# Order of the first loads, split of the strip loads and the number of copy buffers in a fused attention and spline-MLP block

## Chip, cores and metric

The kernel runs on 1 core of one Trainium2 chip. The metric is device time in microseconds (us) of one execution. Before the change three runs took 575.83, 576.78 and 578.7 us, the median is 576.78 us. All data are float32.

## The reference

The block normalizes x (4 batches of 512 tokens, 512 channels) and adds two branches to it. The first is causal attention with 16 heads and a linear position bias. The second is a gated MLP (512 to 2048 to 512) whose three weight matrices are not given densely: each is a cubic interpolation of about 8,000 control points.

```
xn = layernorm(x)
attention: q, k, v = xn @ W + b;  softmax(q k' / sqrt(32) + slope * distance, causal) @ v;  @ Wo + bo
mlp:       gate_w, up_w, down_w = spline(control points)
           inner = silu(xn @ gate_w') * (xn @ up_w')        # 512 -> 2048
           down  = inner @ down_w'                          # 2048 -> 512
out = x + attention + mlp
```

## The kernel before

**Queues.** Every transfer is issued by SyncE (SP), in program order, and `in_order` (L379) fixes the order of all instructions of each engine as written. The transfers take eight semaphores in turn, so transfer n carries a wait for transfer n-8: SP issues it only when that one has landed, and everything behind it on SP waits too.

**Start (L562 to L572, L974 to L997).** `load_x` (L555) loads the four 128-token tiles of the first batch into `xp`, 256 KB each; `load_w` (L452) loads a whole 512x512 weight, 1 MB. SP issues: x tiles 0 and 1, Wv, x tiles 2 and 3, Wq, the bias columns, Wk and more. The first work on the data is written out by hand in L977 to L994. `first_stats` (L714) gives per-token statistics of one tile or two: `moments_of` (two VectorE instructions, L721 and L722), `root` (a VectorE instruction and a ScalarE square root, L726 and L727), `better` (five small VectorE instructions, L731 to L736). `norm` (L740) gives `go` (normalize on VectorE, L745) and `turn_it` (four TensorE transposes, L760, and a ScalarE copy into `xnT`, L761). `value(0, 0)` (`v0`, L797) multiplies token tile 0 by Wv in four steps c over the input channels (L807), two of them before the second tile is turned and two after it. Then q and k of the first heads follow (`project`, L767, matmuls at L776).

**Middle.** Attention of all four batches follows (about 20 us to 408 us). It also builds the MLP weights from control points, and it writes what the MLP needs of the normalized x to DRAM: sampled rows (`samples`) and moments of the stretches between them (`moments`).

**MLP stage (from about 408 us).** The MLP works on 32-row strips of features. `feat[b]` holds them for batch b and is loaded back from DRAM by `load_feat` (L523): four windows w, each of four strip transfers (11 rows of 4x512 values, L530), and after windows 1 and 3 four moment transfers (10 rows of 4x512, L537), 24 transfers in all. The first half `feat[:, 0]` holds windows 0 and 1, the second windows 2 and 3. Two buffers of `feat` take turns.

The order of the stage is written out as strings, one per batch (`plans`, L1197). Capital letters name steps: F0 and F1 issue the two parts of the strip loads for the next batch; G and U (V is U on the other set of PSUM banks) make a quarter of `gate` and of `inner`; m, R and S finish the batch before (moments of inner, down projection, last sum); L loads `res`, the sum of x and attention, 1 MB (L1146).

```
"F0 G0 P0 U0 F1 P1 G1 P2 U1 P3 G2 V2 G3 V3",
"F0 G0 m0:8 U0 L F1 m8:16 G1 T R0:6 U1 T R6:12 G2 R12:16 U2 S G3 V3",
"F0 G0 m0:8 U0 L F1 m8:16 G1 T R0:6 U1 T R6:12 G2 R12:16 U2 S G3 V3",
"G0 m0:8 U0 L m8:16 G1 T R0:6 U1 T R6:12 G2 R12:16 U2 S G3 V3",
"L M0:12 R0:2 M12:16 T R2:16 S",
```

I call these rows phase 0, 1, 2, 3 and the tail. `gate` (L1071) runs 16 matmuls (L1059) into four banks "g" and four ScalarE activations (L1074). `up` (L1076) runs 16 matmuls, four VectorE products into a tile of pool `intp` (L1081, six buffers), and four GpSimd copies into a tile `made` (L1082, two buffers). From `made` SP then moves every other row back into the other strip's place of `inner` (two transfers of 256 KB, L1086) and a few single rows into `lone` (L1091, L1095). The moments of a batch (`m`, L1106) read `inner` after these transfers have landed. S (`down_moments`, L1168) ends in four VectorE sums with `res` (L1186), which free the four banks "o" that V3 writes next, and in four output transfers (L1187).

Of the kernel before, what the change touches and what calls it, by code (L numbers as in the profile page):

```python
# [12 lines left out]
F32 = mybir.dt.float32  # L13
# [5 lines left out]
P = 128  # L19
B, S, D, H = 4, 512, 512, 16  # L20
# [3 lines left out]
NB = D // P  # L24
# [24 lines left out]
NW, NW4 = 11, 4  # L49
# [155 lines left out]
def window(g, w):  # L205

    return 8 * g + 129 * w - 1
# [187 lines left out]
def block_kernel(  # L395
# [17 lines left out]
    nc = tc.nc  # L413
# [35 lines left out]
    xtp = ctx.enter_context(tc.tile_pool(name="xt", bufs=3))  # L449
    wsb = {}  # L450

    def load_w(name, w, pool):  # L452
        wsb[name] = pool.tile([P, NB, D], F32, name=f"w{name}")
        nc.sync.dma_start(out=wsb[name], in_=w.rearrange("(c p) d -> p c d", p=P))


    bcol = wp.tile([P, 5, NHG], F32, name="bcol")
# [62 lines left out]
                if at == k:  # L520
                    nc.sync.dma_start(out=rows[s], in_=o[half * 64 : (half + 1) * 64])

    def load_feat(b, halves=range(2)):  # L523

        strip = lambda j: feat[b][j * Q32 : (j + 1) * Q32]
        turns = [(0, 2, 1, 3), (1, 3, 0, 2)]
        for w in range(2 * halves[0], 2 * halves[-1] + 2):
            for j in turns[w % 2]:
                rows = samples[b][window(j, w) + 1 :][:P].rearrange("(q r) d -> r q d", q=NB)
                nc.sync.dma_start(  # L530
                    out=strip(j)[w % 2 * NW : (w % 2 + 1) * NW, w // 2], in_=rows[:NW]
                )
            if w % 2:
                rows = moments[b].rearrange("(q r) d -> r q d", q=NB)
                for j in turns[0]:
                    at = (2 * j + w // 2) * 2 * NST
                    nc.sync.dma_start(  # L537
                        out=strip(j)[2 * NW :, w // 2], in_=rows[at : at + 2 * NST]
                    )


    with ExitStack() as att:
        attw = att.enter_context(tc.tile_pool(name="attw", bufs=1))
# [11 lines left out]
        def load_x(b, tiles=range(NB)):  # L555
            if tiles[0] == 0:
                xpt[b] = xpp.tile([P, NB, D], F32, name="xp")
            for t in tiles:
                r = (b * NB + t) * P
                nc.sync.dma_start(out=xpt[b][:, t], in_=xpf[r : r + P, :])  # L560

        for k in range(2):  # L562
            nc.gpsimd.memset(lone[k], 0.0)
            nc.gpsimd.memset(edge[k], 0.0)
        load_x(0, range(2))
        load_w("v", Wvp, attw)
        load_x(0, range(2, NB))
        load_w("q", Wqp, attw)
        nc.sync.dma_start(out=bcol, in_=cols)
# [15 lines left out]
            out=dist[:, S - P :],  # L585
            in_=dist[:, S - P :],
# [127 lines left out]
        def first_stats(t0, n):  # L714


            r = rstd[:, t0 : t0 + n]

            def moments_of(t):
                st = stat.tile([P, 6], F32, name="st")  # L720
                nc.vector.bn_stats(st, xpt[0][:, t])  # L721
                nc.vector.bn_aggr(mean[:, t], st)  # L722

            def root():
                variance[t0] = var = stat.tile([P, NB], F32, name="var")[:, :n]
                nc.vector.tensor_scalar_add(var, mean[:, t0 : t0 + n, 1], EPS)  # L726
                nc.scalar.activation(r, var, AF.Sqrt)  # L727

            def better():
                inv = stat.tile([P, NB], F32, name="inv")[:, :n]  # L730
                nc.vector.reciprocal(inv, r)  # L731
                nw = stat.tile([P, NB], F32, name="nw")[:, :n]
                nc.vector.tensor_tensor(nw, inv, inv, ALU.mult)
                nc.vector.tensor_tensor(nw, nw, variance[t0], ALU.mult)
                nc.vector.tensor_scalar(nw, nw, -0.5, 1.5, ALU.mult, ALU.add)
                nc.vector.tensor_tensor(r, inv, nw, ALU.mult)  # L736

            return *(lambda t=t: moments_of(t) for t in range(t0, t0 + n)), root, better

        def norm(b, t):  # L740
            def go():
                j = b * NB + t
                xn = tp.tile([P, D], F32, name="xn", bufs=2)
                ready[b, t] = xn
                nc.vector.tensor_scalar(  # L745
                    xn,
                    xpt[b][:, t],
                    mean[:, j, 0:1],
                    rstd[:, j : j + 1],
                    ALU.subtract,  # L750
                    ALU.mult,
                )

            def turn_it():
                xn = ready.pop((b, t))
                if t == 0:
                    xnT[b] = xtp.tile([P, NB, S], F32, name="xnT", bufs=2)
                ps = ps_m.tile([P, NB, P], F32, name="mm")
                for cb in range(NB):
                    nc.tensor.transpose(ps[:, cb, :], xn[:, cb * P : (cb + 1) * P], ident)  # L760
                nc.scalar.copy(xnT[b][:, :, t * P : (t + 1) * P], ps)  # L761

            return go, turn_it
# [33 lines left out]
        def value(b, t):  # L797

            ps = []

            def go(chunks=range(NB)):
                if t == 0 and chunks[0] == 0:
                    vals[b] = vp.tile([P, NB, D], F32, name="v")
                if chunks[0] == 0:
                    ps.append(ps_m.tile([P, D], F32, name="mm"))
                for c in chunks:
                    nc.tensor.matmul(  # L807
                        ps[0],
                        lhsT=xnT[b][:, c, t * P : (t + 1) * P],
                        rhs=wsb["v"][:, c, :],  # L810
                        start=(c == 0),
                        stop=(c == NB - 1),
                    )
                if chunks[-1] == NB - 1:
                    nc.vector.tensor_copy(vals[b][:, t, :], ps[0])

            return go
# [159 lines left out]
        one, two, three = first_stats(0, 1), first_stats(1, 1), first_stats(2, 2)  # L977
        norms = [norm(0, t) for t in range(NB)]
        v0, q0, k0 = value(0, 0), project("q", 0, 0, 2), project("k", 0, 0, 2)
        for step in (one[0], one[1], two[0], one[2], norms[0][0], two[1], norms[0][1]):  # L980
            step()
        v0(range(2))
        for step in (two[2], norms[1][0], *three[:3], norms[1][1]):
# [61 lines left out]
    featp = ctx.enter_context(tc.tile_pool(name="feat", bufs=1))  # L1045
    midp = ctx.enter_context(tc.tile_pool(name="midp", bufs=1))
    actp = ctx.enter_context(tc.tile_pool(name="actp", bufs=NB + 1))
    madep = ctx.enter_context(tc.tile_pool(name="made", bufs=2))
    intp = ctx.enter_context(tc.tile_pool(name="intp", bufs=6))
    ps_g = ctx.enter_context(tc.tile_pool(name="ps_g", bufs=NB, space=PSUM))  # L1050
    ps_o = ctx.enter_context(tc.tile_pool(name="ps_o", bufs=NB, space=PSUM))

# [18 lines left out]
    def gate(b, q):  # L1071
        for k, ps in enumerate(product(b, q, 0, ps_g, "g")):
            acts[k] = actp.tile([P, S], F32, name="act")
            nc.scalar.activation(acts[k], ps, AF.Silu)  # L1074
# [56 lines left out]
    def add_moments(b, n):  # L1131

        u, t, turned, steps = around[b]
        if not turning[b]:
            turning[b] = True
            for k in range(NB - 1, 0, -1):
                nc.scalar.copy(turned[:ND, k], t[ND:, k])
                nc.scalar.copy(turned[ND:, k], t[:ND, k])
        for k, part in [steps.popleft() for _ in range(min(n, len(steps)))]:
            e = NE - 1 - k  # L1140
            nc.vector.tensor_tensor(u[e][:ND], u[e + 1][:ND], part[:ND], ALU.add)
            nc.vector.tensor_tensor(u[k][ND:], u[k - 1][ND:], part[ND:], ALU.add)
# [62 lines left out]
    def carry_out(b, steps):  # L1205
        for step in steps.split():
            kind, which = step[0], step[1:]
            tiles = range(*map(int, which.split(":"))) if ":" in which else None
            if kind == "G":
                gate(b, int(which))  # L1210
            elif kind == "U":
                up(b, int(which))
            elif kind == "V":
                up(b, int(which), ps_o, "o")
            elif kind == "P":
                last[int(which)][1]()
                if int(which) == 0:
                    last[3][0]()
            elif kind == "M":
                inner_moments(b - 1, tiles, ps_g, "g")  # L1220
            elif kind == "m":
                inner_moments(b - 1, tiles, ps_o, "o")
            elif kind == "F":
                if int(which) == 0:
                    feat[b + 1] = (keep if b % 2 else featp).tile([P, 2, NB, S], F32, name="feat")
                load_feat(b + 1, [int(which)])
            elif kind == "T":
                add_moments(b - 1, 3)
            elif kind == "R":
                down_values(b - 1, tiles, ps_o, "o")  # L1230
            elif kind == "L":
                load_res(b - 1)
            else:
                down_moments(b - 1)

    for b, steps in enumerate(plans):
        carry_out(b, steps)
# [47 lines left out]
```

## Time and profile before

| | |
|---|---|
| runs, median (lowest to highest) | 576.78 us (575.83 to 578.7) |
| profiled execution, its own time | 573.35 us |
| its span from first to last instruction | 571.6 us |
| VectorE busy | 355.3 us (62%) |
| ScalarE busy | 295.8 us (52%) |
| GpSimd busy | 184.8 us (32%) |
| granted TensorE clock | 1.0 |
| transfers | 67.73 MB, mean 118 GB/s |

The profile is one execution. Its time is 573.35 us, 3.4 us below the median of the runs; 1.75 us of it lie outside the span. Times in the views are us from the start of the span. In the timeline a row gives start, length, engine, line, operation, tiles and count; `[idle before <-releaser]` gives how long the engine had stood and what ended it. fp32 matmuls appear as two records each. The trace also holds the moment at which every part of a transfer raised its semaphore; where I say that a transfer landed, it is the last of these.

### The profile page before, as it was taken

How to read it: one execution, taken by the hardware profiler on the slowest of the kernel's cores; microseconds unless marked ns; L12 is line 12 of the kernel's file. 1: busy time of each engine (PE TensorE's matmuls, PEld its weight loads, DVE VectorE, ACT ScalarE, POOL GpSimd, SP SyncE). 2: the span in 40 equal slices, each digit the busy share in tenths (PEclk: the TensorE clock that was granted, in tenths of full speed). 3: DMA queues.
4: the chain of work that ended last, by engine and by line, in shares of the span. 5: the costliest groups of instructions: out<-in, count | busy, mean ns of one | idle time of the engine just before them, and what ended most of it. 6: DMA issues, size and time to landing. Idle time of an engine off the chain costs nothing.

```text
span 571.6 us, 11202 instructions
## 1 busy us (share of the span) xinstructions
PE 560.7 (98%) x4012; PEld 276.7 (48%) x4012; DVE 355.3 (62%) x990; ACT 295.8 (52%) x782; POOL 184.8 (32%) x332
## 2 busy tenths in 40 slices
PE   6999999999999999999999999999999999999997
PEld 4645554544455555444655555555535334333343
DVE  5169998897587785637554545556244573854746
ACT  2366766565357556554756576677514412623323
POOL 2034534253134343222422442443124133113220
PEclk9999999999999999999999999999999999999999
DMA  8942346316453640211020004703546575785344
GB/s 285 344 91 75 73 127 192 108 40 204 128 158 110 193 160 0 66 38 75 2 76 18 1 2 94 128 1 85 129 131 172 119 187 189 130 194 187 115 151 162
DMA packets 34344, 67.73 MB, mean 118 GB/s; under 512 B 5648, under 2 KB 5648, under 8 KB 33776
## 3 DMA queue, kind: packets, MB, share of 16 engines
q1 hardware_dynamic: 34288, 67.01, 41.7%
q8 instruction: 32, 0.52, 0.4%
q14 instruction: 24, 0.20, 0.1%
HBM read 42.35 MB, written 15.29 MB: 101 GB/s over the span
## 4 chain that ended last, share of the span: by engine, by line
PE 87%; DVE 5%; ACT 4%; DMA 3%; issue 1%; SPq 1%; DVEq 0%
PE mm L776 18%; PE mm L891 11%; PE mm L807 10%; PE g L1059 9%; PE mm L475 7%; PE s L834 7%; PE o L1160 6%; PE c L905 5%; PE o L1106 3%; PE o L1177 3%; PE o L475 3%; ACT p L863 2%; PE mm L503 2%; PE o L1059 2%; DMA wv<-in_Wvp_dram 1%; DVE p L847 1%
## 5 line engine op out<-in xcount | busy, mean ns | idle before, releaser
L878 POOL TENSOR_SCALAR p<-p,inv 128x128 f32<-128x128 f32 (+3 forms) x256 | 142.5, 576 | 257.0 <-DVE inv L876 246.8
L863 ACT ACTIVATE p<-p,low 128x128 f32<-128x128 f32 (+3 forms) x256 | 140.7, 552 | 45.9 <-DVE low L847 45.5
L847 DVE CUSTOM_DVE_ANT_0 p<-s,dist 128x128 f32<-128x128 f32 (+3 forms) x256 | 109.2, 482 | 36.2 <-PE s L834 35.3
L891 PEld LDWEIGHTS mm<-ident,p 128*128 128x128 f32 x640 | 71.0, 141 | 40.4 <-issue 25.5
L891 PE MATMUL mm<-ident,p 128*128 128x128 f32 x640 | 89.0, 278 | 1.2 <-ACT pT L896 0.7
L896 ACT COPY pT<-mm 128x512 f32<-128x512 f32 x96 | 55.3, 581 | 53.9 <-PE mm L891 53.6
L1082 POOL COPY made<-inner 128x512 f32<-128x512 f32 x64 | 38.9, 636 | 108.7 <-DVE inner L1081 65.1
L1074 ACT ACTIVATE act<-g 128x512 f32<-128x512 f32 x64 | 33.2, 602 | 61.5 <-PE g L1059 61.5
L807 PE MATMUL mm<-wv,xnT 128*128 128x512 f32 x128 | 58.1, 595 | 2.3 <-DMA wv<-in_Wvp_dram 2.3
L776 PE MATMUL mm<-xnT,wk 128*128 128x512 f32 (+1 forms) x136 | 59.3, 579 | 0.2 <-ACT xnT L761 0.2
L776 PE MATMUL mm<-xnT,wq 128*128 128x512 f32 (+1 forms) x136 | 58.0, 569 | 0.3 <-ACT pT L896 0.2
L1059 PE MATMUL g<-feat,wT 32*128 32x512 f32 x432 | 57.9, 611 | 0.0
L834 PE MATMUL s<-kT,qT 32*128 32x512 f32 (+3 forms) x512 | 51.1, 468 | 0.3
L894 DVE COPY pT<-mm 128x512 f32<-128x512 f32 x64 | 43.6, 687 | 9.1 <-PE mm L891 8.6
L863 ACT ACTIVATION_READ_ACCUMULATOR p<-p,low 128x1 f32 x256 | 48.4, 189 | 0.0
L1081 DVE TENSOR_TENSOR inner<-g,act 128x512 f32<-128x512 f32 x44 | 27.3, 683 | 31.3 <-issue 15.2
L475 PE MATMUL mm<-ctxT,wo 128*128 128x512 f32 x88 | 40.0, 597 | 0.0
L1059 PEld LDWEIGHTS g<-feat,wT 32*128 32x128 f32 x432 | 23.4, 184 | 32.0 <-issue 19.3
L905 PE MATMUL c<-pT,v 128*32 128x128 f32 (+3 forms) x512 | 37.8, 436 | 0.0
L776 PEld LDWEIGHTS mm<-xnT,wk 128*128 128x128 f32 x136 | 24.5, 189 | 25.3 <-issue 21.9
L776 PEld LDWEIGHTS mm<-xnT,wq 128*128 128x128 f32 x136 | 24.7, 190 | 23.5 <-issue 22.3
L807 PEld LDWEIGHTS mm<-wv,xnT 128*128 128x128 f32 x128 | 23.0, 190 | 26.1 <-issue 26.0
(100 smaller groups left out, 556.0 us busy)
## 6 DMA issues: line engine op xcount, KB each, us to landing
inner<-made SPq DMA_DIRECT2D x32, 256.0 KB
feat<-samples SPq DMA_DIRECT2D x64, 88.0 KB
xp<-in_xp_dram SPq DMA_DIRECT2D x16, 256.0 KB
samples<-xnT SPq DMA_DIRECT2D x4, 1024.0 KB
feat<-in_coef_dram SPq DMA_DIRECT2D x8, 512.0 KB
feat<-in_rowpts_dram SPq DMA_DIRECT2D x32, 128.0 KB
xt<-in_xT_dram SPq DMA_DIRECT2D x16, 256.0 KB
mid<-xt SPq DMA_DIRECT2D x16, 256.0 KB
```

The source lines that it names most:

```text
L475: nc.tensor.matmul(ps, lhsT=wsb["o"][:, c, r * P : (r + 1) * P], rhs=ctxT[b][:, c, :], start=(c == 0), stop=(c == NB - 1),)
L776: nc.tensor.matmul(ps[0][:, tokens], lhsT=wsb[name][:, c, hg * P : (hg + 1) * P], rhs=xnT[b][:, c, tokens], start=(c == 0), stop=(c == NB ...
L807: nc.tensor.matmul(ps[0], lhsT=xnT[b][:, c, t * P : (t + 1) * P], rhs=wsb["v"][:, c, :], start=(c == 0), stop=(c == NB - 1),)
L834: nc.tensor.matmul(banks[b, hg][j][:, at : at + (k + 1) * P], lhsT=qk[b, hg, "q"][rows, k * P : (k + 1) * P], rhs=qk[b, hg, "k"][rows, : ( ...
L847: nc.vector.tensor_tensor_reduce(out=p[:, j, :nk], in0=ps[j], in1=dist[:, S - nk :], scale=-SLOPES[hg * NG + j], scalar=BIG, op0=ALU.add, ...
L863: nc.scalar.activation(p[:, j, :nk], p[:, j, :nk], AF.Exp, bias=low[:, j : j + 1], scale=-1.0, accum_out=total[:, j : j + 1],)
L878: nc.gpsimd.tensor_scalar(p[:, j, :nk], p[:, j, :nk], inv[:, j : j + 1], 1.0, ALU.mult, ALU.mult)
L891: nc.tensor.transpose(ps[:, j, :], p[:, j, c * P : (c + 1) * P], ident)
L894: nc.vector.tensor_copy(out, ps)
L896: nc.scalar.copy(out, ps)
L905: nc.tensor.matmul(ps[j * HD : (j + 1) * HD, c * P :], lhsT=vals[b][:, c, hg * P + j * HD : hg * P + (j + 1) * HD], rhs=w[:, j, :], start= ...
L1059: nc.tensor.matmul(ps[k], lhsT=wT[rows, q, 2 * w + part, :], rhs=feat[b][rows, part, q, :], start=(part == 0), stop=(part == 1),)
```

## The change

Three things change. The first loads come in another order: x tile 0, the first half of Wv (input channels 0 to 255), x tile 1, the second half of Wv, x tiles 2 and 3, Wq and so on; the hand-written first VectorE work finishes tile 0 before it begins tile 1. The strip loads of a batch are split in windows 0, 1, 2 (F0: 16 transfers instead of 12) and window 3 (F1: 8 instead of 12). `made` gets a third buffer and `intp` five instead of six; both tiles are of one size.

```diff
-    def load_w(name, w, pool):
-        wsb[name] = pool.tile([P, NB, D], F32, name=f"w{name}")
-        nc.sync.dma_start(out=wsb[name], in_=w.rearrange("(c p) d -> p c d", p=P))
+    def load_w(name, w, pool, chunks=slice(0, NB)):
+        if chunks.start == 0:
+            wsb[name] = pool.tile([P, NB, D], F32, name=f"w{name}")
+        rows = w.rearrange("(c p) d -> p c d", p=P)
+        nc.sync.dma_start(out=wsb[name][:, chunks], in_=rows[:, chunks])
...
-    def load_feat(b, halves=range(2)):
+    def load_feat(b, windows=range(NW4)):
...
-        for w in range(2 * halves[0], 2 * halves[-1] + 2):
+        for w in windows:
...
-        load_x(0, range(2))
-        load_w("v", Wvp, attw)
+        load_x(0, range(1))
+        load_w("v", Wvp, attw, slice(0, 2))
+        load_x(0, range(1, 2))
+        load_w("v", Wvp, attw, slice(2, NB))
         load_x(0, range(2, NB))
...
-        for step in (one[0], one[1], two[0], one[2], norms[0][0], two[1], norms[0][1]):
+        for step in (*one, norms[0][0], *two[:2], norms[0][1]):
...
-    madep = ctx.enter_context(tc.tile_pool(name="made", bufs=2))
-    intp = ctx.enter_context(tc.tile_pool(name="intp", bufs=6))
+    madep = ctx.enter_context(tc.tile_pool(name="made", bufs=3))
+    intp = ctx.enter_context(tc.tile_pool(name="intp", bufs=5))
...
-                load_feat(b + 1, [int(which)])
+                load_feat(b + 1, (range(NW4 - 1), [NW4 - 1])[int(which)])
```

## The prediction

> **What bounds the kernel.** I read the page's busy shares first, then the PE timeline of the two places that the change touches, then the timelines of what ended PE's waits there.
>
> ```profile
> PE 560.7 (98%) x4012; PEld 276.7 (48%) x4012; DVE 355.3 (62%) x990; ACT 295.8 (52%) x782; POOL 184.8 (32%) x332
> ```
>
> TensorE (PE) runs 98% of the span and the chain that ended last lies on it for 87%. So the change can gain only where PE stands or drips, and can lose wherever it makes PE stand. PE at the start:
>
> ```profile
> 9.84 1.96 PE L807 MATMUL mm<-wv,xnT 128*128 128x512 f32 x4 [2.30 <-DMA wv<-in_Wvp_dram]
> 11.63 0.60 PE L760 MATMUL mm<-ident,xn 128*128 128x128 f32 x4
> 12.07 1.88 PE L807 MATMUL mm<-wv,xnT 128*128 128x512 f32 x4
> ...
> 13.91 1.97 PE L776 MATMUL mm<-xnT,wq 128*128 128x256 f32 x8
> ```
>
> PE waits for Wv until 9.8 and then runs without a gap. By the landing events, x tile 0 landed at 3.49, x1 at 4.13, Wv at 9.71, x2 at 10.38, x3 at 11.06, **Wq at 13.78** and Wk at 16.54. In the MLP stage:
>
> ```profile
> 469.52 2.00 PE L1059 MATMUL g<-feat,wT 32*128 32x512 f32 x16
> 471.35 1.90 PE L1059 MATMUL o<-feat,wT 32*128 32x512 f32 x16
> 473.06 2.58 PE L1059 MATMUL g<-feat,wT 32*128 32x512 f32 x16
> 475.57 4.03 PE L1106 MATMUL o<-inner,basist 32*64 32x512 f32 x64
> ...
> 483.71 2.65 PE L1106 MATMUL o<-inner,basist 32*64 32x512 f32 x32 [0.28 <-DMA inner<-made]
> ...
> 505.88 2.00 PE L1059 MATMUL g<-feat,wT 32*128 32x512 f32 x16
> 507.95 3.34 PE L1059 MATMUL o<-feat,wT 32*128 32x512 f32 x15
> ...
> 511.14 3.61 PE L1059 MATMUL g<-feat,wT 32*128 32x512 f32 x13
> 514.67 3.69 PE L1106 MATMUL o<-inner,basist 32*64 32x512 f32 x64
> ...
> 520.22 4.37 PE L1106 MATMUL o<-inner,basist 32*64 32x512 f32 x64
> ```
>
> An undisturbed group of 16 takes 1.72 to 1.93, one of 64 takes 3.62. So G3, V3, G0 (505.88 to 514.67 = 8.8, undisturbed 5.4) lose 3.4 at the end of phase 2, and 0.6 at the end of phase 1 (469.52 to 475.57). The matmuls m8:16 lose 1.2 in phase 2 (481.46 to 486.30) and 0.7 in phase 3 (520.22 to 524.52). That is all the change can reach there: 5.9. What ended these waits:
>
> ```profile
> 499.06 0.40 SPq L1146 DMA_DIRECT2D res<-mid  x1
> 499.50 7.92 SPq L530 DMA_DIRECT2D feat<-samples  x8
> 507.47 1.47 SPq L537 DMA_DIRECT2D feat<-moments  x4
> ...
> 517.70 2.13 SPq L1086 DMA_DIRECT2D inner<-made  x2
> ```
> ```profile
> 507.20 2.48 DVE L1186 TENSOR_TENSOR res<-o,res 128x512 f32<-128x512 f32 x4 [2.18 <-issue]
> ```
>
> Three transfers end them. **res**, issued at 499.06, lands at 507.12; L1186 starts at 507.20 and frees the banks of V3 one by one. **The last strip** of F1 lands at 513.52, and G0 ends 1.15 later (end of phase 1: 474.25, G0 ends at 475.57). **V3's inner<-made** lands last, at 522.58 (phase 2: 484.35, issued 479.05), and the second half of m8:16 needs it. SP is held by the rule of eight: the first seven F1 strips are out by 502.3, the eighth waits for res and leaves at 507.14; everything behind it on SP, down to V3's inner<-made, comes later for that.
>
> **Start.** One transfer more; SP spends 0.43 on it (L454's row), which nothing waits for, since transfers land later than issued. Bytes ahead of Wq are the same, so I leave Wq at 13.78. Tile 0's VectorE chain loses the second tile's bn_stats (0.68) ahead of it, but ScalarE keeps its order: the square root of x1 stands before the copy of tile 0. So v0 now needs x1, which lies behind 512 KB of Wv. A straight line between 4.13 and 9.71 puts x1 at 6.9; if the slow spell of the first Wv packets stays whole ahead of it, it lands at 8.4 (9.71 less 1.3 for 512 KB at 390 GB/s, the pace of x2 to x3). From x tile to v0 is 2.1 in this trace (3.49 to the square root's end at 4.85, copy 0.59, semaphores), so v0 starts at 9.0 to 10.5, and PE is ready for q 4.07 later, at 13.1 to 14.6. Wq holds q to about 13.85. What is gained on Wv is lost on Wq: -0.05 at one end, +0.7 at the other. I take **+0.1**, near the middle (x1 at 7.7). A trace with another slow spell could move this by some tenths either way.
>
> **Strips, 16 and 8.** Count and bytes are unchanged: 24 transfers, 88 KB and 80 KB. In phase 2 the first seven strips land from 490.08 to 494.59, 0.75 apart; that is the pace of the queue. Four of them now stand ahead of U0's six transfers and of res, on SP and in the queue.
>
> - *res.* It is the 23rd transfer after F0 starts and waits for the 15th: 490.08 + 14 x 0.75 = 500.5, plus 0.7 which inner<-made costs the strips beside it (12 took 8.9 where 11 steps of 0.75 are 8.2): issued at 501.2, 2.1 later. But before, the queue ran dry while res was on its way:
>
> ```profile
> 499.00:500.50 1.50, 1.50 (x36) 0.44 (x24) 1.12 (x2) 0.76 (x2) 0.00 (x0) 1.00 0.55 109
> 501.00:503.00 2.00, 2.00 (x20) 0.65 (x14) 0.46 (x1) 0.00 (x0) 0.00 (x0) 1.00 0.91 373
> ```
> (the last two columns are the DMA share and GB/s). Now strips and inner fill that hole until about 503, and res follows at 2.5 (8 packets of 0.31 on each engine): 505.5, or 507.7 if one engine lags by 2.2 as it did (504.93 the second last, 507.12 the last). L1186 stays where it was within 0.6.
> - *Last strip.* Behind res stand 8 strips, not 12: 505.5 + 8 x 0.72 (their pace before: 12 from 504.9 to 513.52) = 511.3, plus up to 1.1 because U1's inner<-made now comes beside more of them. I take 512.4, the old time less the hole: **-1.1** at G0 of phase 3. In phase 1 the queue had no such hole; only the dip at 469.5 to 471.5 (DMA share 0.51) goes: **-0.5**. Bounds: nothing, and the 0.6 and 3.4 above.
> - *SP.* Only the eighth strip after res waits for it, and that is now the last of F1. In phase 1 U1's transfers start at about 468.3 instead of 470.22; V3's inner<-made, nine transfers and four outputs behind, is issued near 477 instead of 479.05. m8:16 needs it at 482.7: **-1.2** in phase 2; in the same way **-0.7** in phase 3. Bounds: nothing, and these.
> - *Phase 0.* F0's four extra transfers delay P0's store and with it the load of xt for P3 (issued 417.98) by 2.3; P3 reads it at 430.8, so it costs nothing. Strips of F1 land before 435.43; G0 runs at 438.
>
> **Third made buffer.** GpSimd's copy for V3 waits 9.69 (at 515.39) for U1's transfers to leave the shared buffer. SP takes V3's transfers at 517.70, when its own row was free at 517.45: 0.2 alone, and counted above. Five `intp` buffers cost nothing: U1 takes the tile that R0:6 read just ahead of it on PE.
>
> **Sum:** 0.1 - 0.5 - 1.2 - 1.1 - 0.7 = -3.4. Against the profiled 573.35 that is 569.95; against the median of the runs, 3.4 higher, 576.8 - 3.4 = **573.4**.
>
> **Rivals.**
> 1. *Slower: res lands four strips later.* Then the queue keeps its order and the hole stays: +3.0 (4 x 0.75) on res. For it: strips after res all landed behind it; res took 8.06 from issue in phase 2, 7.34 in phase 1. Against it: the hole. It decides once res slips over 1.5 in phase 1 (landed 467.03, L1186 began 468.58) and from the first tenth in phase 2. V3 then drips with L1186: G0 +0.6 and +1.3, SP behind res +0.2, start +0.7: +2.8, **579.6**. [...]
> 2. *No change.* The pace of the strips, not their split, sets the last landing, and SP's chain of 0.75 per transfer sets V3's inner<-made; only the 0.2 of the buffer and the dip remain, and the start takes them: **576.5**.
> 3. *More.* V3's whole drip goes too (res before 505) and Wq lands earlier for a shorter slow spell: 5.9 + 0.3 - 0.2 = -6.0, **570.8**.
>
> **Chances.** Forecast 0.50 (own range 571.5 to 575.5), no change 0.22, slower 0.18, more 0.10. Half a per cent, 2.9, is about what a measurement of this kernel can tell from no change. Beyond it lies 0.56 of the forecast and all of rival 3: faster 0.38. Slower gets two thirds of rival 1, with 0.02 for worse starts: 0.14. The rest, 0.48, is within. The range takes rivals 2 and 3 and part of 1: 570.8 to 578.5.
>
> **What would show it.** v0 (L807) starts at 9.0 to 10.5, ended by ScalarE's copy, not by Wv, and q's first matmul at 13.85. SP issues res about 2 later against F0's first strip, and U1's inner<-made right behind its landing. The second half of m8:16 follows the first without a gap. G3 to G0's end takes 5.5 in phase 1 and 7.7 in phase 2. The forecast is wrong if L1186 starts later against S than before, or if v0 starts after 10.5.

## The result and the profile after

| | kernel before | changed kernel |
|---|---|---|
| runs side by side | 22 | 22 |
| median (lowest to highest), us | 576.4 (570.68 to 579.98) | 572.41 (568.13 to 576.39) |
| ratio of the times, 95% interval | 1 | 0.9934 (0.9909 to 0.9958) |

The change makes the kernel 0.66% faster, 3.8 us of 576.4, with an interval of 2.4 to 5.2 us. The forecast was 3.4 us. Runs more than 1.5% above the fastest of their kernel count in no ratio and in no mean of the granted clock, here and below.

The profiled execution of the changed kernel is no picture of that gain: its own time is 576.39 us, the highest of its 22 runs, and 3.0 us *above* the profiled execution of before (573.35). Whoever subtracts the two profiles reads a loss. What made this one execution so long is the first thing to find. First its shares and its row of granted TensorE clock (one digit for each fortieth of the span):

```profile
PE 563.5 (98%) x4012; PEld 277.7 (48%) x4012; DVE 355.6 (62%) x990; ACT 295.8 (51%) x782; POOL 184.2 (32%) x332
...
PEclk8999999999999999999999999999999999999999
```

TensorE's (PE's) share is the same and its busy time is 2.8 us longer, with the same 4012 instructions. The first digit says where: 8 instead of 9. Here is the PE timeline of the start.

```profile
9.42 3.65 PE L811 MATMUL mm<-wv,xnT 128*128 128x512 f32 x4 [2.35 <-ACT xnT L765]
12.90 0.60 PE L764 MATMUL mm<-ident,xn 128*128 128x128 f32 x4
13.34 1.88 PE L811 MATMUL mm<-wv,xnT 128*128 128x512 f32 x4
...
15.06 1.89 PE L780 MATMUL mm<-xnT,wq 128*128 128x256 f32 x8
```

v0 starts at 9.42, ended by ScalarE's copy, as forecast. But its first four matmul records take 3.65, the next four 1.88. The view by stretches gives the granted clock of each stretch (the first column is its length, then busy time of PE, PEld, DVE, ACT, POOL, then the clock, the DMA share and GB/s):

```profile
5.98:9.39 3.41, 1.09 (x9) 0.74 (x7) 1.81 (x7) 0.68 (x2) 0.00 (x0) 1.00 1.02 382
9.39:12.80 3.41, 3.38 (x4) 1.41 (x5) 2.90 (x11) 0.20 (x1) 0.00 (x0) 0.50 1.06 388
```

In 5.98 to 9.39 PE is busy for 1.09 of 3.41 us; in the next 3.41 us it gets half its clock (0.50), and v0 pays for it. The profiled execution of before, with PE busy for 1.75 and 1.86 of 3.41 in the like places, shows the full clock throughout (1.00). Neither the forecast nor its rivals knew of this.

The end of phases 1 and 2, PE and then the four sums of S (VectorE):

```profile
470.61 2.00 PE L1063 MATMUL g<-feat,wT 32*128 32x512 f32 x16
472.43 3.23 PE L1063 MATMUL o<-feat,wT 32*128 32x512 f32 x15
...
475.50 3.22 PE L1063 MATMUL g<-feat,wT 32*128 32x512 f32 x13
478.65 3.69 PE L1110 MATMUL o<-inner,basist 32*64 32x512 f32 x64
...
484.20 1.97 PE L1110 MATMUL o<-inner,basist 32*64 32x512 f32 x32
486.89 2.55 PE L1110 MATMUL o<-inner,basist 32*64 32x512 f32 x32 [0.71 <-DMA inner<-made]
...
508.95 2.00 PE L1063 MATMUL g<-feat,wT 32*128 32x512 f32 x16
511.78 3.34 PE L1063 MATMUL o<-feat,wT 32*128 32x512 f32 x15 [0.83 <-DVE res L1190]
...
514.97 3.28 PE L1063 MATMUL g<-feat,wT 32*128 32x512 f32 x13
518.19 3.69 PE L1110 MATMUL o<-inner,basist 32*64 32x512 f32 x64
...
523.73 3.90 PE L1110 MATMUL o<-inner,basist 32*64 32x512 f32 x64
```
```profile
471.57 2.48 DVE L1190 TENSOR_TENSOR res<-o,res 128x512 f32<-128x512 f32 x4 [1.82 <-DMA res<-mid]
...
511.03 2.49 DVE L1190 TENSOR_TENSOR res<-o,res 128x512 f32<-128x512 f32 x4 [2.94 <-PE g L1063]
```

From G3's start to G0's end: 470.61 to 478.65, 8.0 us (before 6.05, forecast 5.5), and 508.95 to 518.19, 9.2 us (before 8.8, forecast 7.7). In phase 1 the sums now wait for `res`, until 471.57 where G3 had already begun at 470.61, and V3 drips behind them; that is what rival 1 described. m8:16 has its gap in phase 2 still (0.71) and has lost it in phase 3 (3.90). So this one execution seems to refute the forecast at both phase ends and in m8:16 of phase 2, and yet the kernel is as fast as forecast. The experiments have to say where the gain lies.

### The profile page after: what moved, and what is told of

Its sections match the earlier page's. It is cut to its first block, busy times and chain, and to the rows that moved or that the text cites. A ratio compares the mean times of both kernels' runs of the same rounds, so it can differ in the third digit from the quotient of the medians.

```text
span 574.6 us, 11201 instructions
## 1 busy us (share of the span) xinstructions
PE 563.5 (98%) x4012; PEld 277.7 (48%) x4012; DVE 355.6 (62%) x990; ACT 295.8 (51%) x782; POOL 184.2 (32%) x332
## 4 chain that ended last, share of the span: by engine, by line
PE 84%; DVE 5%; DMA 5%; ACT 4%; SPq 1%; issue 1%; POOL 0%; DVEq 0%
PE mm L780 18%; PE mm L895 11%; PE mm L811 10%; PE g L1063 7%; PE mm L477 7%; PE s L838 7%; PE c L909 5%; PE o L1164 5%; PE o L1110 3%; PE o L477 3%; ACT p L867 2%; PE o L1181 2%; PE mm L505 2%; DMA inner<-made 2%; PE o L1063 2%; DVE p L851 1%
## 5 line engine op out<-in xcount | busy, mean ns | idle before, releaser
L811 PE MATMUL mm<-wv,xnT 128*128 128x512 f32 x128 | 59.8, 610 | 2.3 <-ACT xnT L765 2.3
L780 PEld LDWEIGHTS mm<-xnT,wq 128*128 128x128 f32 x136 | 24.7, 190 | 23.2 <-issue 22.0
```

What stands on the lines that cost most here:

```text
L780: nc.tensor.matmul(ps[0][:, tokens], lhsT=wsb[name][:, c, hg * P : (hg + 1) * P], rhs=xnT[b][:, c, tokens], start=(c == 0), stop=(c == NB ...
L811: nc.tensor.matmul(ps[0], lhsT=xnT[b][:, c, t * P : (t + 1) * P], rhs=wsb["v"][:, c, :], start=(c == 0), stop=(c == NB - 1),)
```

## The experiments

Each kernel ran in turn with the kernel before on the same chip; the ratio is to that kernel. Besides the time, each run lists its mean granted clock. Since the clock in all fourteen profiles is 1.0 or 0.5 and nothing between, 2 x (1 - clock) x span is the **half-clock time** of a run: for the profiled run of the changed kernel 2 x 0.003 x 574.6 = 3.4, which is its one stretch of 3.41. The clock is listed to 0.001, so one run's value is good to about 0.6 us.

| kernel | runs | median us | ratio (95%) | half-clock us, mean of runs |
|---|---|---|---|---|
| before, beside the first four | 35 | 576.7 | 1 | 5.1 |
| loads | 12 | 574.33 | 0.998 (0.9947 to 1.0013) | 5.3 |
| strips | 12 | 573.48 | 0.996 (0.9929 to 0.999) | 1.5 |
| buffer | 12 | 576.49 | 1.0003 (0.997 to 1.0036) | 7.7 |
| strips_buffer | 12 | 574.8 | 0.9969 (0.9932 to 1.0006) | 4.5 |
| before, beside the next four | 19 | 577.35 | 1 | 8.2 |
| after2 | 6 | 571.73 | 0.9903 (0.9866 to 0.994) | 0.8 |
| warm | 7 | 572.55 | 0.9925 (0.9898 to 0.9952) | 2.5 |
| resfirst | 9 | 573.17 | 0.9911 (0.9878 to 0.9943) | 3.6 |
| warm_resfirst | 10 | 573.03 | 0.9922 (0.9894 to 0.9949) | 3.8 |
| before, beside the last four | 17 | 578.03 | 1 | 9.9 |
| busy_old | 12 | 575.17 | 0.9954 (0.9929 to 0.9978) | 4.1 |
| busy_new | 6 | 573.52 | 0.9907 (0.9873 to 0.9941) | 1.5 |

The changed kernel's 22 runs have 1.8 us of half clock in the mean.

**One part at a time.** `loads` has only the new order of the first loads, `strips` only the new split, `buffer` only the third copy buffer, `strips_buffer` all but the first loads.

```diff
# loads
-        load_x(0, range(2))
-        load_w("v", Wvp, attw)
+        load_x(0, range(1))
+        load_w("v", Wvp, attw, slice(0, 2))
+        load_x(0, range(1, 2))
+        load_w("v", Wvp, attw, slice(2, NB))
# strips
-                load_feat(b + 1, [int(which)])
+                load_feat(b + 1, (range(NW4 - 1), [NW4 - 1])[int(which)])
# buffer
-    madep = ctx.enter_context(tc.tile_pool(name="made", bufs=2))
-    intp = ctx.enter_context(tc.tile_pool(name="intp", bufs=6))
+    madep = ctx.enter_context(tc.tile_pool(name="made", bufs=3))
+    intp = ctx.enter_context(tc.tile_pool(name="intp", bufs=5))
```

> Only the new order of the first loads, with the two halves of Wv and the reordered first VectorE work. Theory 1 (the gain of 3.8 us lies in the strip split): v0 starts near 9.4, q near 13.4, no more than 0.6 us gained where the TensorE clock stays whole, and up to 1.1 us lost where it is halved for 3.4 us as in the changed kernel's profile; median within 1 us of before. Theory 2 (the gain lies in the start, the MLP stage of the changed kernel's profile being slower is its true cost): 3 us or more faster than before. Theory 3 (third buffer): no change.

> Only the split of the strip loads, 16 and 8. Theory 1: 2 to 3.5 us faster than before, from the ends of phases 1 and 2 (G3 to G0's end) and from m8:16. Theory 2: slower by 1 to 2 us, as the MLP stage of the changed kernel's profile is (408.45 to 571.6 before, 409.53 to 574.6 after). Theory 3 (the third buffer is what lets V3's transfers leave early): no change without the buffer.

> Only three made buffers and five intp buffers. Theory 1: 0 to 0.3 us faster, since SP takes V3's transfers in its own order (517.70 when SP was free at 517.45). Theory 2: no change. Theory 3: GpSimd's wait of 9.7 us before V3's copies was the cause of m8:16's stall, 1 to 2 us faster.

> Strip split and third buffer together, first loads as before. Theory 1: 2.5 to 4 us faster, nearly all of the change. Theory 2: 1 to 2 us slower than before. Theory 3: 1 to 2 us faster, no more than the buffer alone.

The split carries most: 0.4%, 2.3 us. The first loads give 0.2%, 1.2 us, with an interval that takes in nothing. The buffer alone gives nothing. `strips_buffer` gives 1.8 us, short of the 2.5 to 4 expected, with an interval that just takes in nothing. It is not better than `strips`; their intervals overlap almost wholly, and its half-clock time is three times as long.

In the table the split stands out in the last column too: 1.5 us of half clock where before has 5.1. The PE timeline of `loads` (old split) and of `strips` (new split) at the end of phase 1 shows what halved clock costs:

```profile
471.62 2.40 PE L1063 MATMUL g<-feat,wT 32*128 32x512 f32 x10
474.60 2.04 PE L1063 MATMUL g<-feat,wT 32*128 32x512 f32 x6 [0.57 <-DMA feat<-moments]
476.56 5.09 PE L1110 MATMUL o<-inner,basist 32*64 32x512 f32 x64
```
```profile
473.05 3.02 PE L1059 MATMUL g<-feat,wT 32*128 32x512 f32 x16
476.00 3.69 PE L1106 MATMUL o<-inner,basist 32*64 32x512 f32 x64
```

In `loads` G0 drips with the last strips, and the 64 matmul records of m0:8 behind it take 5.09. In `strips` they take 3.69. The stretches of `loads`:

```profile
472.64:476.06 3.42, 2.85 (x12) 0.95 (x8) 1.81 (x4) 0.91 (x2) 0.00 (x0) 1.00 0.95 202
476.06:479.47 3.41, 3.41 (x33) 1.14 (x40) 0.00 (x0) 1.27 (x3) 2.01 (x4) 0.50 0.75 275
```

After a stretch in which PE waits for strips, the clock is halved for 3.41 us, though PE is busy for 2.85 of 3.42 us there by its records. By their number that is too long: the stretch holds 12 of them, and 16 take 1.72 to 1.93 us where nothing waits, so 12 would take about 1.4. The rest must be waiting that the records hold.

**The changed kernel again, with its two visible waits taken out.** `after2` is the changed kernel once more. `warm` puts ten matmuls of the identity between tile 0's transposes and v0, `resfirst` issues L ahead of F0 in phases 1 and 2, `warm_resfirst` does both.

```diff
# warm
+        awake = ps_m.tile([P, NB, P], F32, name="mm")
+        for k in range(10):
+            nc.tensor.matmul(awake[:, k % NB, :], lhsT=ident, rhs=ident, start=True, stop=True)
# resfirst (both rows)
-        "F0 G0 m0:8 U0 L F1 m8:16 G1 T R0:6 U1 T R6:12 G2 R12:16 U2 S G3 V3",
+        "L F0 G0 m0:8 U0 F1 m8:16 G1 T R0:6 U1 T R6:12 G2 R12:16 U2 S G3 V3",
```

> The changed kernel once more, as the base of the three beside it and for a second profile. Theory 1 (the gain has two parts: fewer us at half TensorE clock, and a shorter end of phases 1 and 2): a ratio near 0.993 again, the mean of half-clock time per run near 1.8 us against about 5 of the kernel before, and q starting 0.13 us after Wq lands. Rival (the gain comes from the start alone): the same ratio, but half-clock time no different from before.

> The changed kernel with ten more identity matmuls (20 records, some 2 us) between the turning of tile 0 and v0, so that TensorE has work while it waits for tile 1. Theory 1: the half-clock window at 9.4 of the changed kernel's profile goes, 0.5 to 1 us off the mean; the windows at the ends of phases stay. Rival (the half clock there is chance and not idle time): the same share of runs at 0.997 and no gain.

> The changed kernel with the load of res moved ahead of the strips in phases 1 and 2 (L before F0). Theory 1: L1186 no longer waits for res, V3 runs without dripping (1.9 instead of 3.3), G3 to G0's end is bound by the last strip alone, 0.5 to 2 us faster, and fewer half-clock windows near 476 and 514. Rival (the last strip alone sets the end of the phase): V3 runs earlier but G0 ends no earlier, no gain.

> Both edits on the changed kernel. Theory 1: their gains add, 1 to 3 us under the changed kernel. Rival: no gain from either.

None of the three beats `after2`; all intervals overlap. In `after2` the half clock is nearly gone without any help (0.8 us), and the start of its profile runs as it should:

```profile
9.12 1.99 PE L811 MATMUL mm<-wv,xnT 128*128 128x512 f32 x4 [1.54 <-ACT xnT L765]
10.94 0.60 PE L764 MATMUL mm<-ident,xn 128*128 128x128 f32 x4
11.38 1.88 PE L811 MATMUL mm<-wv,xnT 128*128 128x512 f32 x4
13.10 1.89 PE L780 MATMUL mm<-xnT,wq 128*128 128x256 f32 x8
```

So there was little left for `warm` to save; its own runs have 2.5 us of half clock. `resfirst` did what it was to do: the sums of S start at S's end and V3 no longer drips. Here is PE at its end of phase 1:

```profile
469.97 1.90 PE L1063 MATMUL o<-feat,wT 32*128 32x512 f32 x16
471.69 1.88 PE L1063 MATMUL g<-feat,wT 32*128 32x512 f32 x10
473.76 1.43 PE L1063 MATMUL g<-feat,wT 32*128 32x512 f32 x6 [0.20 <-DMA feat<-moments]
475.12 3.69 PE L1110 MATMUL o<-inner,basist 32*64 32x512 f32 x64
```

V3 is whole (1.90), and G0 waits in its place. By the landing events G0's end stays 1.1 to 1.2 behind the last strip, at both phase ends of this profile and of the changed kernel's. So the last strip ends the phase, and V3's drip lies beside it: the late `res` of rival 1 has no cost that these runs show. They would not show one well below 2 us, the half width of their intervals, and `resfirst` has 3.6 us of half clock where `after2` has 0.8.

**The start alone.** `front_old` and `front_new` leave out the whole MLP stage and the last projections and write the last batch's attention context four times; the first has the old order of the first loads, the second the new.

```diff
     last = [proj(B - 1, r, ps_o, "o") for r in range(NB)]
-    for load, _ in last[:3]:
-        load()
...
-    for b, steps in enumerate(plans):
-        carry_out(b, steps)
+    for b in range(B):
+        t = midp.tile([P, NB, S], F32, name="res")
+        nc.vector.tensor_copy(t, ctxT[B - 1])
+        nc.sync.dma_start(out=out[b].rearrange("(c p) s -> p c s", p=P), in_=t)
```

> The kernel before with the MLP stage left out: the phases are not run, the last projections are not made, and the output is the last batch's attention context, stored four times. It is the base for front_new. Theory 1 (new loads make Wq land about 1 us earlier, and q starts right behind it): this one is slower than front_new by 0.7 to 1.2 us. Rival (the start gains nothing, since what is gained on Wv is lost on Wq): both within 0.3 us.

> The changed kernel with the same stage left out, so that only the order of the first loads and of the first VectorE work differs from front_old. Theory 1: 0.7 to 1.2 us faster than front_old, Wq landing between 12.2 and 13 against 13.6 to 14.6, and q 0.13 to 0.5 behind it. Rival: within 0.3 us of front_old.

The medians are 435.97 us (5 runs, 433.36 to 436.68) and 433.57 us (4 runs, 433.32 to 435.83), the means 435.26 and 434.07: the new order is 1.2 to 2.4 us faster, on few runs. The PE timelines, old and new:

```profile
10.18 2.64 PE L807 MATMUL mm<-wv,xnT 128*128 128x512 f32 x4 [2.55 <-DMA wv<-in_Wvp_dram]
...
15.81 1.89 PE L776 MATMUL mm<-xnT,wq 128*128 128x256 f32 x8
```
```profile
8.93 1.98 PE L811 MATMUL mm<-wv,xnT 128*128 128x512 f32 x4 [2.04 <-ACT xnT L765]
...
12.91 1.89 PE L780 MATMUL mm<-xnT,wq 128*128 128x256 f32 x8
```

q starts 2.9 us earlier. Part of that is the clock: in `front_old` it is halved from 11.31 to 14.73, through most of v0. The rest is Wq, which lands at 14.13 in the one and at 12.43 in the other.

The clock also stands behind most of the difference in time. Both kernels list a clock of 0.970 to 0.978, because it is halved for their last 20.8 us, where PE has nothing left to do. One more stretch of 3.41 us lowers the listed clock by 0.004. Three of the five runs of `front_old` list 0.970 to 0.972, and one of the four of `front_new` lists 0.972. The others, at 0.975 and more, take 433.8 us in the mean of two with the old order and 433.5 in the mean of three with the new one: 0.3 us apart. So on these few runs the new order gains mainly by meeting the half clock less often.

**Is the half clock the cause?** If waiting PE loses its clock, then PE kept busy must gain, although it does more. `busy_old` is the kernel before, `busy_new` the changed one, each with 8 matmuls of the identity ahead of G0 in phases 2 and 3, where PE stands.

```diff
+        if b >= 2 and q == 0 and w == 0:
+            for k in range(2 * NB):
+                nc.tensor.matmul(ps[k % NB][:, :P], lhsT=ident, rhs=ident, start=True, stop=True)
```

> The kernel before with eight identity matmuls (16 records, 1.7 us) ahead of G0's product in phases 2 and 3, where TensorE waits for the last strip; they write banks that the product overwrites. Theory 1 (idle TensorE time at the ends of phases 1 and 2 halves the clock, and that is part of the cost of late strips): half-clock time falls from some 6 us to under 3, and the time by 1 to 2 us although work is added. Rival (half-clock windows come whatever TensorE does there): the same half-clock time, and 0 to 3 us slower for the added work.

> The same eight matmuls in the changed kernel. Theory 1: little half-clock time is left to gain (0.8 to 1.8 us per run), so the time is within 1 us of the changed kernel. Rival: 1 to 3 us slower than the changed kernel.

PE in `busy_old` at the end of phase 1 (16 records for the 8 added matmuls):

```profile
476.12 2.05 PE L1058 MATMUL g<-ident 128*128 128x128 f32 x16
478.10 2.59 PE L1062 MATMUL g<-feat,wT 32*128 32x512 f32 x16
480.62 3.69 PE L1109 MATMUL o<-inner,basist 32*64 32x512 f32 x64
```

The added work puts about 2 us into each of two waits and makes the old kernel 0.46% *faster* (interval 0.22% to 0.71%), with 4.1 instead of 9.9 us of half clock; under 3 were expected. In the changed kernel, whose half clock is small already, six runs show no difference: 0.9907 beside 0.9903 for `after2`.

## Why the forecast's total was right and its terms were not

The sum was right (3.4 forecast, 3.8 measured), and that it was is in good part luck. The start's term had the wrong sign, the last strip's 1.6 did not come, SP's 1.9 is not shown in its size, and a cause that was not in the sum makes up part of the gain, 1.4 us by the estimate below. Times below are landing events and PE rows of single executions of the kernels with the old or the new part; these differ by a microsecond and more (Wq landed at 11.54 to 12.96 in eight executions of the new order), so a mean of several is given where there are several.

The forecast also named a sign by which it would be wrong: L1186 starting later against S than before. By that sign it was wrong. In the changed kernel's profile the sums start 1.9 us later against S at the end of phase 1 and 0.8 later at the end of phase 2, and in `after2` 0.5 later at the end of phase 2. It did not cost the total, as far as `resfirst` can tell, because the last strip ends these phases.

**Start: +0.1 forecast; about -1.2 measured, with an interval that takes in nothing** (`loads`). The failed step is "Bytes ahead of Wq are the same, so I leave Wq at 13.78". v0 came as forecast or earlier (8.2 to 9.6 in eight executions, 9.0 to 10.5 forecast; x1 landed at 5.4 to 7.5, ahead of the 7.7 taken). But Wq landed at 13.73 in the mean of six executions of the old order (12.24 to 14.56) and at 12.41 in the mean of eight of the new one (11.54 to 12.96). In before, five of the sixteen parts of Wq land more than 1 us behind the rest (eleven from 11.51 to 12.44, five from 13.56 to 13.78), a lag that shows already at Wv (eleven by 8.08, five from 9.49). How many are late differs: one in `strips`, none in `strips_buffer`, where Wq lands at 12.24. From the first part to the last it is 1.2 to 3.3 us in the old order and 0.8 to 1.7 in the new one. So equal bytes ahead did not mean equal time here. Where the clock is whole at the start, q starts at 13.40 in the mean of three profiles of the old order and at 12.82 in the mean of seven of the new one, 0.6 earlier. With the 0.3 of the front pair at like clock, what the order gains by itself is nearer to half a microsecond than to 1.2; the runs do not settle it.

**Last strip: -0.5 and -1.1 forecast, 0 measured.** The step was "I take 512.4, the old time less the hole". From F0's first issue to the last strip's landing it takes 26.1 us in the mean of three executions with the old split (both phases; 25.1 to 27.8) and 26.2 in the mean of five with the new (24.7 to 28.1). Whatever became of the hole in the queue, the last strip came no earlier; here rival 2's "The pace of the strips, not their split" was right. From the start of S's last four matmuls to m0:8, both phases together, the mean is 18.3 us with the old split and 17.7 in seven executions with the new, and single executions lie from 16.75 to 20.0.

**SP: -1.2 and -0.7 forecast, not shown in that size.** U1's `inner<-made` is issued behind `res` and ahead of the rest as forecast, and in `strips` it leaves at 469.24 where before had 470.22, 1.0 earlier where 1.9 was forecast. It lands no earlier (476.42, before 475.53), and m8:16 waits for V3's, and in `strips` these leave at 479.28, no earlier than the 479.05 of before. GpSimd and SP in `strips`:

```profile
476.98 2.28 POOL L1082 COPY made<-inner 128x512 f32<-128x512 f32 x4 [7.65 <-DMA lone<-made]
...
476.48 1.81 SPq L1187 DMA_DIRECT2D out_dram<-res  x4
479.28 1.41 SPq L1086 DMA_DIRECT2D inner<-made  x2
```

SP has issued the outputs by 478.29. It waits for GpSimd's copies of V3, which end at 479.26, because they began only when U1's last transfer out of the shared `made` buffer had landed, at 476.83. With three buffers the copies end 1.2 to 3.5 us ahead of the issue in four profiles, and V3's transfers then leave 2.16 (`after2`), 2.54 (`warm`), 3.01 (`strips_buffer`) and 3.46 us (the changed kernel's profile, where V3 itself is late behind `res`) after the start of m0:8; before had 3.48. At the end of phase 2 of `strips` it is the same: the copies end at 517.26, the transfers leave at 517.29. So SP's step works only together with the third buffer, which the sum gave "0.2 alone, and counted above", and then in some executions and not in others.

What it is worth in time stays open. From m0:8 to the start of S's last four matmuls, without executions whose clock was halved there, phase 2 takes 29.35 in the one execution of before and 28.69 in the mean of five with the new split (28.24 to 29.34), phase 3 takes 28.65 (mean of two) and 28.18 (mean of four). That would be -0.66 and -0.47. But `busy_old`, which has the old split and two buffers, takes 28.22 and 27.80 there, so executions of the old split differ by as much.

**Third buffer: 0.2, counted in the above. Measured alone: nothing** (1.0003). Beside the split it lets V3's copies go early, as shown; no run shows a gain in time from that.

**What the forecast lacked: the granted clock.** Over the runs of the kernel before, the time rises by 0.35 to 0.43 us with each microsecond of half clock (three sets of 16 to 33 runs); at the listed 0.50 it would be 0.5 for a PE that always has work, by an estimate. In `loads` the halved stretch begins at 476.06, half a microsecond before m0:8, while G0 still drips with the strips, and m0:8 takes 1.4 more (5.09 against 3.69) for these 3.41 us, 0.41 for each. Taking 0.43 and 5.1 less 1.8 us of half clock, the clock gives 1.4 us by this estimate. The runs at full clock (0.999 or more) give the remainder: 573.3 in the mean of 9 runs of before and 570.9 of 13 of the changed kernel, 2.4 us. The sum, 3.8, is the measured gain, but these two sets did not run side by side, and the runs of before beside the changed kernel list no clock, so the agreement to a tenth is luck. Which parts of the change make up the 2.4 is not shown. At full clock `loads` lies 0.9 below before (3 runs), `strips` 0.2 (8 runs), `buffer` 0.5 (3 runs) and `strips_buffer` 2.0 (4 runs), and single runs of one kernel differ by more than that.

The half clock comes in pieces of like length: every stretch inside the kernels was 3.41 or 6.83 us. How many there are differs from run to run: the kernel before lists 1.0 to 0.991 in the runs of one set, mostly in steps of 0.003, which is one such stretch in 574.5 us. At the end of the front pair it stands behind an idle PE: PE is idle for the whole of 410.67 to 414.08 in `front_old`, and the clock is halved from 414.08. Inside the kernels a whole idle stretch did not come before it: PE was busy for 1.09 of 3.41 us ahead of one and, by its records, for 2.85 of 3.42 ahead of another.

An estimate from the rows tells what these stretches have in common. Count each matmul record at the pace that its group has where nothing waits (0.43 us for one of v0, 0.11 for one of G and U, 0.06 for one of m), instead of its recorded length. Then the eleven stretches right before a halving inside the kernels of all fourteen profiles hold 0.5 to 1.4 us of work each. Of the 2181 other whole stretches at full clock, laid off in steps of 3.41 us from the first listed one, five hold as little, four of them the first one that a profile lists. Three more, at the end of phase 2 in `strips`, `after2` and the changed kernel's profile, hold 1.5 or 1.6, and none of them is followed by a halving. So in these profiles, by this estimate, halvings followed on stretches with 0.5 to 1.4 us of work and on none with 1.5 or more; the five that hold as little and are followed by none are not explained. The 8 matmuls added in each wait of `busy_old` are 16 records of 0.11, 1.7 us of work.

**Rivals.** 1 (slower): its mechanism is in the changed kernel's profile (the sums wait for `res` until 471.57, and V3 behind them takes 3.23), its price is not found, as far as `resfirst` can tell. Its "strips after res all landed behind it" holds for phase 1 of the kernel before (`res` at 467.03, the next strip at 467.64); in phase 2 three of them landed from 505.38 to 506.95, ahead of `res` at 507.12. 2 (no change): right on the strips, wrong on the total. 3 (more): its "Wq lands earlier for a shorter slow spell" is what happened, and Wq moved by 1.3 where 0.3 was given; how much of that reaches the total is open.

**What stays open.** Where the 2.4 us at full clock come from. Whether the new split meets the half clock less often only because it shortens the waits at the phases' ends by 0.6 us in the mean; and why `strips_buffer` has 4.5 us of it where `strips` has 1.5 and the changed kernel 1.8. Ten to twenty runs of each do not settle that. At the start, halved stretches lie in 3 of 6 profiles of the old order and in 1 of 8 of the new one, which is suggestive and no more. Why the new order shortens the lag of Wq's last parts was not tried apart.

## What to carry to other kernels

A right total can stand on wrong terms: only parts run alone showed that. Before two single profiles are compared, look at the granted clock of each and at where its own time lies among the runs; here they differed by +3.0 us where the kernels differ by -3.8. A wait on the busiest engine is priced at its length and at what the profile shows of that engine's clock after it (here 0.50 for 3.41 us behind G0's wait in `loads`); whether this counts can be tried cheaply by filling the wait with work that nobody needs (here 8 matmuls in each of two waits, 2.7 us faster). When a transfer is to leave earlier, look for everything that it waits for: here the engine that issues it was free at 478.29, and the copy that fills its buffer was not done until 479.26 (`strips`).

## What the runs showed of the hardware

- Inside the kernels TensorE's granted clock was 0.50 for 3.41 or 6.83 us after a stretch of 3.41 us in which TensorE had little work, by estimate 0.5 to 1.4 us of it (eleven cases): 64 matmul records that take 3.69 (`strips`) took 5.09 (`loads`), four that take 1.98 (`front_new`) took 3.65 (the changed kernel's profile). It came in some executions and not in others of the same kernel: 0.8 to 9.9 us per run in the mean of a set, and differing between sets of the same kernel (5.1, 8.2, 9.9 for before).
- More TensorE work made a kernel faster: 8 added matmuls in each of two waits took 2.7 us off the kernel before (0.46% of 578).
- The order of the first loads moved the landing of a later load of 1 MB by 1.3 us with the same bytes ahead of it (13.73 in the mean of six profiles, 12.41 in the mean of eight).
- A moved transfer was visibly late and cost nothing that shows: `res` held the sums of S back by 1.9 us in the changed kernel's profile (469.65 to 471.57), and in `resfirst`, where it does not, the time is no better (0.9911 beside 0.9903).
